# Where four per-sample norms are made: beside the attention windows or inside the spectra

## The chip, the cores and the metric

The kernel runs on one core of one Trainium2 chip. Its time is the device time of one execution, in microseconds (us): the median of 3 runs is 3876.3 us (3873.66 to 3883.53). The profiled execution has a span of 3873.3 us.

The core's engines each work through their own list of instructions and wait for one another through semaphores: TensorE (PE, matrix products), VectorE (DVE), ScalarE (ACT), GpSimd (POOL), and SyncE (SP), which issues most of the DMA transfers.

## The reference, cut to what matters

The program is a stack of four layers on an image tensor of 4 samples, 56 x 56 pixels, 128 channels. Layer 2 is a neural operator on the 56 x 56 token x channel images of each sample. It starts with two nested normalisations, a group norm over the sample (`_gn`, 32 groups of 4 channels) and an instance norm over the pixels of one image (`_inorm`), and then takes Fourier transforms of the normed images:

```python
x = x + _L0_conv_ref(_gn(x), ...)   # window attention, global attention, MLP
x = x + _L1_conv_ref(_gn(x), ...)   # edge layer
x = x + _L2_conv_ref(_gn(x), ...)   # spectral attention: the norms of this text
x = x + _L3_conv_ref(_gn(x), ...)

def _gn(v, G=32, eps=1e-5):
    g = v.reshape(B_, H_, W_, G, C_ // G)
    m = jnp.mean(g, axis=(1, 2, 4), keepdims=True)
    s = jnp.var(g, axis=(1, 2, 4), keepdims=True)
    return ((g - m) / jnp.sqrt(s + eps)).reshape(v.shape)

# in layer 2
def _inorm(x, g, b):
    m = jnp.mean(x, axis=(-2, -1), keepdims=True)
    v = jnp.var(x, axis=(-2, -1), keepdims=True)
    return (x - m) * jax.lax.rsqrt(v + EPS) * g + b
...
    xa_n = _inorm(xa, norm_g[0], norm_b[0])
    k = _fno_layer(xa_n, wK, wKs, bKs, (H // 2, W // 2))   # rfft2 of the image, products, irfft2
    q = _fno_layer(xa_n, wQ, wQs, bQs, (H // 2, W // 2))
    v = _fno_layer(xa_n, wV, wVs, bVs, (H, W))
```

## The kernel before

Layers 0 and 1 are computed for one sample after the other: 7x7 windows (`fast_windows`), global attention, MLP, edge layer. Their result of a sample stands in the tile x1 and is stored to x2d in DRAM. Then layer 2 begins for all samples at once, with the spectra. The branch used here is the one for small scores.

The two norms of layer 2 for one sample are a generator. Each `yield` ends one step, so that a caller can lay the steps between its own instructions. `bank()` gives a bank of PSUM, `xad` is the sample's place in DRAM.

```python
    x = xp[:, :HH, :]
    rows = wk.tile([P, HH, 6], F32, name="s_rows", bufs=1)
    for t in range(HH):
        nc.vector.bn_stats(rows[:, t, :], x[:, t, :])
        if t % 2 == 1:
            yield
    mv = wk.tile([P, 2], F32, name="s_mv", bufs=1)
    nc.vector.bn_aggr(mv, rows.rearrange("p a b -> p (a b)"))
    yield
    ps = bank()
    nc.tensor.matmul(ps[:, 0:1], k.g4, mv[:, 0:1], start=True, stop=True)
    yield
    mr = wk.tile([P, 2], F32, name="s_mr", bufs=1)
    t1 = wk.tile([P, 1], F32, name="s_t1", bufs=1)
    nc.vector.tensor_copy(mr[:, 0:1], ps[:, 0:1])
    nc.vector.tensor_sub(t1, mv[:, 0:1], mr[:, 0:1])
    nc.vector.scalar_tensor_tensor(t1, t1, t1, mv[:, 1:2], ALU.mult, ALU.add)
    yield
    ps = bank()
    nc.tensor.matmul(ps[:, 1:2], k.g4, t1, start=True, stop=True)
    yield
    var = wk.tile([P, 1], F32, name="s_var", bufs=1)
    nc.vector.tensor_copy(var, ps[:, 1:2])
    half = [rows[:, :, i] for i in range(6)]
    mean, sq, d = tiny("mean"), tiny("sq"), tiny("d")
    nc.vector.tensor_sub(d, half[1], half[4])
    yield
    nc.vector.tensor_mul(d, d, d)
    nc.vector.tensor_add(sq, half[2], half[5])
    yield
    nc.vector.scalar_tensor_tensor(sq, d, HH / 4, sq, ALU.mult, ALU.add)
    nc.vector.tensor_add(mean, half[1], half[4])
    yield "root"
    nc.scalar.activation(t1, var, AF.Sqrt, bias=k.eps)
    yield
    yield
    nc.vector.reciprocal(mr[:, 1:2], t1)
    nc.vector.tensor_scalar(mean, mean, 0.5, mr[:, 0:1], ALU.mult, ALU.subtract)
    nc.vector.tensor_scalar_mul(mean, mean, mr[:, 1:2])
    yield
    nc.vector.tensor_scalar(sq, sq, mr[:, 1:2], mr[:, 1:2], ALU.mult, ALU.mult)
    ps = bank()
    nc.tensor.matmul(ps[:, 64:64 + HH], k.ones_c, mean, start=True, stop=True)
    yield
    nc.vector.tensor_copy(st.norm[:, b, 0, :], ps[:, 64:64 + HH])
    nc.vector.tensor_sub(d, mean, st.norm[:, b, 0, :])
    yield
    nc.vector.tensor_mul(d, d, d)
    nc.vector.scalar_tensor_tensor(sq, d, float(HH), sq, ALU.mult, ALU.add)
    yield
    ps = bank()
    nc.tensor.matmul(ps[:, 128:128 + HH], k.ones_px, sq, start=True, stop=True)
    yield
    nc.vector.tensor_copy(d, ps[:, 128:128 + HH])
    yield
    for t in range(0, HH, 14):
        apply_norm(k, x[:, t:t + 14, :], x[:, t:t + 14, :], mr)
        if t == 42:
            nc.sync.dma_start(xad, x)
        yield "root" if t == 42 else None
    nc.scalar.activation(d, d, AF.Sqrt, bias=k.eps)
    yield
    yield
    nc.vector.reciprocal(d, d)
    nc.vector.tensor_scalar_mul(st.norm[:, b, 1, :], d, w.ng[:, 0:1])
    yield
```

Here `apply_norm` is one DVE instruction, recorded at line 193 (`tensor_scalar(out, xt, mr[:, 0:1], mr[:, 1:2], subtract, mult)`). The normed image replaces the raw one in place.

Before the change, the windows of sample b carry the steps of the norm of sample b - 1 (`beside` is this generator; a step follows each stage of the windows):

```python
# fast_windows
        steps = beside(bank)
        ...
        for n in range(NG + 11):
            for stage, g in ((norm, n + 2), (project, n), (score, n - 1), (value, n - 2), ...):
                if 0 <= g < NG:
                    stage(g)
                    step(False)
```

The spectra transform each sample along the channels (`first_transform`, four pieces of 14 tokens) and then along the tokens (`sample_spectra`, 13 parts: three s_ps, two blocks for R, eight s_px):

```python
# first_transform
    z = to[b] = wk.tile([P, 33, 2 * HH], F32, name="s_z")
    xf = x.rearrange("p t h -> p (t h)")
    for t0 in range(0, HH, 14):
        ps = psum.tile([P, 512], F32, tag="row", name="s_pr")
        for t in range(14):
            for ri in range(2):
                nc.tensor.matmul(ps[64 * ri:64 * ri + 64, t * 33:(t + 1) * 33],
                                 xf[:, (t0 + t) * HH:(t0 + t) * HH + 64], k.fw[:, ri, :], start=True, stop=True)
        nc.vector.tensor_mul(z[:, :, t0:t0 + 14], ps[:, :462].rearrange("p (t f) -> p f t", t=14),
                             bc(st.norm[:, b, 1, t0:t0 + 14], 1, 33))
        nc.scalar.copy(z[:, :, HH + t0:HH + t0 + 14], z[:, :, t0:t0 + 14])
        yield

# sample_spectra
    for c0, c1, v in C_BLOCKS_S:
        ps = psum.tile([P, 512], F32, tag="acc", bufs=4, name="s_ps")
        m = (c1 - c0) * HH
        nc.tensor.matmul(ps[:, :m].rearrange("p (c t) -> p c t", t=HH), k.fs[:, v, :], z[:, c0:c1, :HH],
                         start=True, stop=True)
        for dst, rows in ((st.S, slice(0, 64)), (st.iS, slice(64, P))):
            nc.scalar.copy(dst[o, b // 2, c0:c1, :HH], ps[rows, :m].rearrange("p (c t) -> p c t", t=HH))
        yield
    ...   # st.apart <- st.S, and two parts that write st.R
    for c0 in range(0, 32, 4):
        ps = psum.tile([P, 512], F32, tag="acc", bufs=4, name="s_px")
        for i in range(4):
            nc.tensor.matmul(ps[:112, i * 112:(i + 1) * 112], z[:, c0 + i, :], k.fx, start=True, stop=True)
        copy(k, c0 // 4, st.xh[:, b, :, c0:c0 + 4, :].rearrange("p i c r -> p c i r"),
             ps[:112, :448].rearrange("p (c i r) -> p c i r", c=4, i=2))
        yield

# spectra
        norm = normed_images(k, w, st, B - 1, wk, lambda: tiny.tile([P, 512], F32, name="s_pt"), st.x1, xad[B - 1])
        zs = {}
        first = [first_transform(k, st, b, (wk, psum), st.x1 if b == B - 1 else images(b), zs) for b in range(B)]
        for _ in first[0]:
            pass
        for b in range(B):
            for n, _ in enumerate(sample_spectra(k, st, b, (wk, psum), zs.pop(b))):
                for _ in range(3):
                    next(norm, None)
                if b < B - 1 and n in (2, 5, 7, 9):
                    next(first[b + 1])
```

The instructions of PE, ACT and DVE stand in the order of the program here. Those of other parts that are outside such a fixed order, like `conv_weights` (small DVE operations on weights, lines 1749 to 1775), are put between them by the program's scheduler.

Of the kernel before, what the change touches and what calls it, by code (L numbers as in the profile page):

```python
# [12 lines left out]
F32 = mybir.dt.float32  # L13
# [3 lines left out]
PSUM = bass.MemoryType.PSUM  # L17
DRAM = bass.MemoryType.DRAM

P = 128  # L20
B = 4
HH = 56
# [1286 lines left out]
def first_transform(k, st, b, pools, x, to):  # L1309

    nc = k.nc
    wk, psum = pools
# [13 lines that stand above are left out]
# [38 lines left out]
def spectra(k, w, st, xad, images):  # L1366

    nc, tc = k.nc, k.tc  # L1370
    for t in (st.S, st.iS, st.R):
        nc.gpsimd.memset(t[:, :, :, HH:], 0.0)
    nc.gpsimd.memset(st.x1[:, HH, :], 0.0)
    with ExitStack() as es:
        wk = es.enter_context(tc.tile_pool(name="s_wk", bufs=2))
        psum = es.enter_context(tc.tile_pool(name="s_ps", bufs=3, space=PSUM))
        tiny = es.enter_context(tc.tile_pool(name="s_pt", bufs=1, space=PSUM))
        es.enter_context(tc.manual_schedule(engines={mybir.EngineType.PE, mybir.EngineType.Activation,
                                                     mybir.EngineType.DVE}))
        norm = normed_images(k, w, st, B - 1, wk, lambda: tiny.tile([P, 512], F32, name="s_pt"), st.x1, xad[B - 1])  # L1380
        zs = {}
        first = [first_transform(k, st, b, (wk, psum), st.x1 if b == B - 1 else images(b), zs) for b in range(B)]
        for _ in first[0]:
            pass
        for b in range(B):
            for n, _ in enumerate(sample_spectra(k, st, b, (wk, psum), zs.pop(b))):
                for _ in range(3):
                    next(norm, None)
                if b < B - 1 and n in (2, 5, 7, 9):
                    next(first[b + 1])  # L1390


def value_weights(k, I, w, wk, dd):
# [1030 lines left out]
def build(k, packs, I, out):  # L2424


    nc, tc = k.nc, k.tc
    with ExitStack() as es:
        cp = es.enter_context(tc.tile_pool(name="const", bufs=1))
        dp = es.enter_context(tc.tile_pool(name="dram", bufs=1, space=DRAM))  # L2430
        x2d = dp.tile([B, P, HH, HH], F32, name="x2d")
        xad = dp.tile([B, P, HH, HH], F32, name="xad")
# [3 lines left out]
        x1w = x1p.tile([P, HH + 1, HH], F32, name="x1")  # L2436
# [4 lines left out]
        st = Env()  # L2441
        st.x1 = x1w
        st.norm = l2p.tile([P, B, 2, HH], F32, name="norm")
        with tc.tile_pool(name="w01", bufs=1) as wp, tc.tile_pool(name="io", bufs=1) as io:
            xw = io.tile([P, TOK], F32, name="xw")
            with ExitStack() as pre:
                xs = pre.enter_context(tc.tile_pool(name="i_x", bufs=B - 1))
                x = [xw] + [xs.tile([P, TOK], F32, name="i_x") for _ in range(B - 1)]
                w0, w1, w2 = Env(), Env(), Env()
# [35 lines left out]

            def norms(b, bank):

                if b < 0:
                    return iter(())
                return normed_images(k, w2, st, b, io, bank, x1w, xad[b])  # L2490

            with tc.If(small_scores > 0) as small:
                for b in range(B):
                    first_layers(lambda *a: fast_attention(*a, functools.partial(norms, b - 1), k.mr[:, b, :]), I["x"][b],
                                 x2d[b] if b < B - 1 else None, loaded=b == 0)
            with small.Else():
                with tc.For_i(0, B, 1) as b:
                    first_layers(functools.partial(both_attentions, beside=None),
                                 I["x"][bass.ds(b, 1)].rearrange("b p t -> (b p) t"),
                                 x2d[bass.ds(b, 1)].rearrange("b p l n -> (b p) l n"))  # L2500
                with tc.tile_pool(name="n_x", bufs=2) as xs, tc.tile_pool(name="n_ps", bufs=2, space=PSUM) as psum:
                    for b in range(B - 1):
                        xp = xs.tile([P, HH, HH], F32, name="n_x")
                        nc.sync.dma_start(xp, x2d[b])
                        for _ in normed_images(k, w2, st, b, io, lambda: psum.tile([P, 512], F32, name="n_ps"), xp,
                                               xad[b]):
                            pass

        x2s = ExitStack()
        x2p = x2s.enter_context(tc.tile_pool(name="x2", bufs=2, side="right"))  # L2510
# [1 line left out]
        def images(b):  # L2512
            if b not in loaded:
                xp = loaded[b] = x2p.tile([P, HH + 1, HH], F32, name="s_x2")
                for t in range(0, HH, 28):
                    nc.sync.dma_start(xp[:, t:t + 28, :], xad[b, :, t:t + 28, :])
                nc.gpsimd.memset(xp[:, HH, :], 0.0)
            return loaded[b]

# [54 lines left out]
```

## Time and profile before

| what | us |
|---|---|
| median of 3 runs | 3876.3 |
| span of the profiled run | 3873.3 |
| PE busy | 3546.0 (92%) |
| DVE busy | 2897.3 (75%) |
| ACT busy | 2077.8 (54%) |
| POOL busy | 1210.6 (31%) |
| windows of sample 0: first w_mm matmul to first f_s matmul | 55.23 to 155.06 |
| windows of sample 1 | 755.07 to 865.03 |
| windows of sample 2 | 1465.06 to 1575.02 |
| windows of sample 3 | 2178.53 to 2288.44 |
| spectra: first s_pr matmul to first q_acc matmul | 2888.70 to 2977.52 |

The names of tiles tell the stages: w_ is the windows, f_ global attention, m_ the MLP, e_ the edge layer, s_ the norms and the spectra, q_ the attention weights of layer 2. A line such as L1322 is the line of the kernel that made an instruction. A granted clock of 1.00 is PE's full speed.

### The profile page before, as it was taken

The page shows a single profiled execution, that of the slowest core. Times are in us where ns is not written, and L with a number is a line of the kernel's source. Part 1 is how long each engine was busy: PE and PEld are TensorE (multiplying, and loading weights), DVE is VectorE, ACT ScalarE, POOL GpSimd, SP SyncE. Part 2 cuts the span into 40 slices and gives each one's busy share as a digit, 9 for nine tenths or more (in the row PEclk, how much of TensorE's full clock was granted, in tenths as well). Part 3 has the DMA queues.
Part 4 walks back from the last instruction along what each step waited for, and adds up shares of the span by engine and source line. Part 5 has one row for each costly group of instructions (what it writes and reads, how often), then busy time and mean ns, then how long its engine had stood idle before and what let it go on. Part 6 is the DMA issues. An engine that isn't in the chain of part 4 may idle for free. (4 is left out here: it accounts for less than half of the span.)

```text
span 3873.3 us, 79430 instructions
## 1 busy us (share of the span) xinstructions
PE 3546.0 (92%) x35416; PEld 1589.1 (41%) x35416; DVE 2897.3 (75%) x2703; ACT 2077.8 (54%) x2080; POOL 1210.6 (31%) x667
## 2 busy tenths in 40 slices
PE   6899999989998998999989989999998989989988
PEld 4422234543322455322245532223456433336654
DVE  6588877859887786688869758887776767765664
ACT  4577765448776554677745457776542012214332
POOL 0000006600000570000028300000655769975555
PEclk8999999999999999999999999999998989998888
DMA  2000000000000000000000000000011058831101
GB/s 96 1 1 1 1 1 19 19 18 1 1 1 1 18 3 34 1 1 1 1 17 3 19 18 1 1 1 34 2 44 49 1 121 170 175 101 59 52 8 50
DMA packets 73496, 111.12 MB, mean 29 GB/s; under 512 B 62140, under 2 KB 63932, under 8 KB 67900
## 3 DMA queue, kind: packets, MB, share of 16 engines
q1 hardware_dynamic: 14460, 93.13, 8.0%
q10 hardware_dynamic: 58688, 12.85, 2.0%
q8 instruction: 279, 4.57, 0.5%
q14 instruction: 69, 0.57, 0.0%
HBM read 79.46 MB, written 26.51 MB: 27 GB/s over the span
## 5 line engine op out<-in xcount | busy, mean ns | idle before, releaser
L663 ACT ACTIVATE f_ring<-f_s 128x1792 f32<-128x1792 f32 (+3 forms) x796 | 1097.3, 1429 | 226.6 <-PE f_s L661 224.8
L606 DVE TENSOR_TENSOR f_acc<-f_acc,f_ring 128x1792 f32<-128x1792 f32 x560 | 1134.1, 2025 | 64.3 <-ACT f_ring L663 7.5
L661 PE MATMUL f_s<-f_qT,f_kT 32*128 32x448 f32 x5376 | 738.3, 572 | 47.9 <-ACT f_ring L663 27.9
L877 POOL TENSOR_TENSOR m_sq<-m_y 128x392 f32<-128x392 f32 x16 | 14.5, 919 | 1975.4 <-ACT m_y L876 1975.3
L612 PE MATMUL f_po<-f_ring,f_va 128*32 128x448 f32 x5376 | 589.8, 546 | 0.0
L1029 DVE TENSOR_TENSOR e_td<-e_pa,e_c 128x1792 f32<-128x1792 f32 x252 | 491.3, 2013 | 14.4 <-ACT e_a L994 14.4
L1031 POOL TENSOR_TENSOR e_tp<-e_a,e_c 128x1792 f32<-128x1792 f32 x140 | 451.8, 3257 | 145.1 <-PE e_acc L1036 104.4
L661 PEld LDWEIGHTS f_s<-f_qT,f_kT 32*128 32x128 f32 x5376 | 268.4, 183 | 524.5 <-ACT f_ring L663 378.9
L1036 PE MATMUL e_acc<-e_td,t_shared 32*32 32x448 f32 x8064 | 323.7, 546 | 22.0 <-DVE e_td L1029 10.9
L1033 ACT ACTIVATE e_tp<-e_tp 128x1792 f32<-128x1792 f32 x140 | 235.1, 1696 | 176.2 <-POOL e_tp L1031 176.2
L1645 DVE TENSOR_TENSOR u_ud<-u_px,u_d 112x1792 f32<-112x1792 f32 x144 | 240.1, 1708 | 96.4 <-PE u_po L1650 87.3
L612 PEld LDWEIGHTS f_po<-f_ring,f_va 128*32 128x32 f32 x5376 | 133.2, 109 | 396.3 <-issue 395.3
L1036 PE MATMUL e_acc<-e_tp,t_shared 32*32 32x448 f32 x4480 | 222.3, 547 | 3.2 <-ACT e_tp L1033 2.5
L1650 PE MATMUL u_po<-u_ud,AT 112*64 112x448 f32 x960 | 201.6, 550 | 23.3 <-DVE u_ud L1645 23.3
L1647 POOL TENSOR_TENSOR u_up<-xh,u_d 112x1792 f32<-112x1792 f32 x64 | 193.8, 3054 | 25.7 <-PE u_po L1650 12.4
L1036 PEld LDWEIGHTS e_acc<-e_td,t_shared 32*32 32x32 f32 x8064 | 134.1, 103 | 146.4 <-DVE e_td L1029 56.0
L629 DVE RECIPROCAL f_den<-f_den 128x448 f32<-128x448 f32 x28 | 82.7, 2953 | 77.2 <-ACT f_den L628 77.2
L1650 PE MATMUL u_po<-u_up,AT 112*64 112x448 f32 x576 | 126.9, 548 | 0.2
L1650 PEld LDWEIGHTS u_po<-u_ud,AT 112*64 112x64 f32 x960 | 64.9, 137 | 147.9 <-issue 86.7
L606 DVE TENSOR_TENSOR f_acc<-f_ring 128x1792 f32<-128x1792 f32 x28 | 56.7, 2025 | 86.6 <-ACT f_ring L663 57.7
L1512 POOL TENSOR_TENSOR q_u<-iS,q_g 128x1792 f32<-128x1792 f32 x32 | 102.7, 3237 | 56.2 <-PE s_px L1360 33.4
L1036 PEld LDWEIGHTS e_acc<-e_tp,t_shared 32*32 32x32 f32 x4480 | 95.2, 103 | 55.3 <-ACT e_tp L1033 19.4
(485 smaller groups left out, 4797.0 us busy)
## 6 DMA issues: line engine op xcount, KB each, us to landing
u_d<-dd SPq DMA_DIRECT2D x48, 784.0 KB
xw<-in_x SPq DMA_DIRECT2D x4, 1568.0 KB
x2d<-x SPq DMA_DIRECT2D x4, 1568.0 KB
xad<-x SPq DMA_DIRECT2D x4, 1568.0 KB
x_xs<-xad ACTq DMA_DIRECT2D x32, 196.0 KB
xm<-x_ev ACTq DMA_DIRECT2D x64, 98.0 KB
o_a<-xm SPq DMA_DIRECT2D x8, 784.0 KB
o_x<-x2d SPq DMA_DIRECT2D x4, 1568.0 KB
```

The costliest lines, as they stand in the source:

```text
L606: nc.vector.tensor_add(acc, slots(j, 0) if c == 1 else acc, slots(j, c))
L612: nc.tensor.matmul(po[heads[h], :NB], va[o, c, heads[h]], p, start=(c == 0), stop=(c == 24))
L661: nc.tensor.matmul(ss[:, i, :NB], kT[heads[h], c * P:(c + 1) * P], qT[heads[h], blk(j)], start=True, stop=True)
L663: nc.scalar.activation(ring[:, slot:slot + m, :], ss[:, :m, :NB], AF.Exp, scale=scale)
L1029: nc.vector.tensor_tensor(t, am, cm, ALU.max)
L1031: nc.gpsimd.tensor_sub(t, bc(a.rearrange("p (l n) -> p l n", l=8), 1, 4), cm)
L1033: nc.scalar.activation(tf, tf, AF.Relu)
L1036: nc.tensor.matmul(acc[quarters[q], r, :NB], k.ident[o, o], t[o, q].rearrange("p l n -> p (l n)"), start=(g == 0), stop=(g == len(EDGE_TUR ...
L1512: nc.gpsimd.tensor_mul(u, bc(st.iS[:, bp, c, :HH], 1, HEADS), bc(g[:, n, c, :], 2, HH))
L1645: nc.vector.tensor_mul(u, bc(px[:, :, :NB], 2, m), dm)
L1647: nc.gpsimd.tensor_mul(u, bc(x, 2, m), dm)
L1650: nc.tensor.matmul(po[64 * b2:64 * b2 + 64, :NB], st.AT[:, 8 * i + h0 + q, 2 * bp + b2, :], u[:, b2, q, :], start=(left == 16), stop=(left ...
```

## The change

The norms of samples 1, 2 and 3 move. Only the norm of sample 0 stays beside windows, those of sample 1. The other three are made inside the spectra, which now take the samples in the order 0, 3, 1, 2, so that sample 3, whose raw image still stands in x1, comes early, and each norm can be made in small steps while the sample before it is transformed. Three steps follow each piece of the first transform of sample 0, four follow each of the 13 parts of a sample; the first transform of the next sample moves from parts 2, 5, 7, 9 to parts 8 to 11, and ahead of it the norm that it needs is finished. Samples 1 and 2 are loaded raw from x2d rather than normed from xad, and are normed in place and stored to xad from there. It is meant to take the norms away from stages that they may hold up and to lay them where other work leaves room.

```diff
--- before.py
+++ after.py
@@ -1377,17 +1377,33 @@
         tiny = es.enter_context(tc.tile_pool(name="s_pt", bufs=1, space=PSUM))
         es.enter_context(tc.manual_schedule(engines={mybir.EngineType.PE, mybir.EngineType.Activation,
                                                      mybir.EngineType.DVE}))
-        norm = normed_images(k, w, st, B - 1, wk, lambda: tiny.tile([P, 512], F32, name="s_pt"), st.x1, xad[B - 1])
+
+
+        order = [0, B - 1, *range(1, B - 1)]
+
+        def of(b):
+            return st.x1 if b == B - 1 else images(b)
+
+        def steps(n):
+            for norm in norms[:1]:
+                for _ in range(n):
+                    if next(norm, norm) is norm:
+                        norms.pop(0)
+                        break
+
+        norms = [normed_images(k, w, st, b, wk, lambda: tiny.tile([P, 512], F32, name="s_pt"), of(b), xad[b])
+                 for b in order[1:]]
         zs = {}
-        first = [first_transform(k, st, b, (wk, psum), st.x1 if b == B - 1 else images(b), zs) for b in range(B)]
+        first = [first_transform(k, st, b, (wk, psum), of(b), zs) for b in order]
         for _ in first[0]:
-            pass
-        for b in range(B):
+            steps(3)
+        for i, b in enumerate(order):
             for n, _ in enumerate(sample_spectra(k, st, b, (wk, psum), zs.pop(b))):
-                for _ in range(3):
-                    next(norm, None)
-                if b < B - 1 and n in (2, 5, 7, 9):
-                    next(first[b + 1])
+                if i < B - 1 and 8 <= n < 12:
+                    while n == 8 and len(norms) + i >= B - 1:
+                        steps(1)
+                    next(first[i + 1])
+                steps(4)
 
 
 def value_weights(k, I, w, wk, dd):
@@ -2485,26 +2501,24 @@
 
             def norms(b, bank):
 
-                if b < 0:
+                if b != 1:
                     return iter(())
-                return normed_images(k, w2, st, b, io, bank, x1w, xad[b])
+                return normed_images(k, w2, st, 0, io, bank, x1w, xad[0])
 
             with tc.If(small_scores > 0) as small:
                 for b in range(B):
-                    first_layers(lambda *a: fast_attention(*a, functools.partial(norms, b - 1), k.mr[:, b, :]), I["x"][b],
+                    first_layers(lambda *a: fast_attention(*a, functools.partial(norms, b), k.mr[:, b, :]), I["x"][b],
                                  x2d[b] if b < B - 1 else None, loaded=b == 0)
             with small.Else():
                 with tc.For_i(0, B, 1) as b:
                     first_layers(functools.partial(both_attentions, beside=None),
                                  I["x"][bass.ds(b, 1)].rearrange("b p t -> (b p) t"),
                                  x2d[bass.ds(b, 1)].rearrange("b p l n -> (b p) l n"))
-                with tc.tile_pool(name="n_x", bufs=2) as xs, tc.tile_pool(name="n_ps", bufs=2, space=PSUM) as psum:
-                    for b in range(B - 1):
-                        xp = xs.tile([P, HH, HH], F32, name="n_x")
-                        nc.sync.dma_start(xp, x2d[b])
-                        for _ in normed_images(k, w2, st, b, io, lambda: psum.tile([P, 512], F32, name="n_ps"), xp,
-                                               xad[b]):
-                            pass
+                with tc.tile_pool(name="n_x", bufs=1) as xs, tc.tile_pool(name="n_ps", bufs=2, space=PSUM) as psum:
+                    xp = xs.tile([P, HH, HH], F32, name="n_x")
+                    nc.sync.dma_start(xp, x2d[0])
+                    for _ in normed_images(k, w2, st, 0, io, lambda: psum.tile([P, 512], F32, name="n_ps"), xp, xad[0]):
+                        pass
 
         x2s = ExitStack()
         x2p = x2s.enter_context(tc.tile_pool(name="x2", bufs=2, side="right"))
@@ -2513,7 +2527,7 @@
             if b not in loaded:
                 xp = loaded[b] = x2p.tile([P, HH + 1, HH], F32, name="s_x2")
                 for t in range(0, HH, 28):
-                    nc.sync.dma_start(xp[:, t:t + 28, :], xad[b, :, t:t + 28, :])
+                    nc.sync.dma_start(xp[:, t:t + 28, :], (x2d if b else xad)[b, :, t:t + 28, :])
                 nc.gpsimd.memset(xp[:, HH, :], 0.0)
             return loaded[b]
```

The last hunk is in `images(b)`, which loads a sample into one of two tiles for the spectra. The branch after `small.Else()` isn't the one that runs here.

## The prediction

> **What bounds the kernel now.** I read the page first: TensorE (PE) is busy 92% of the span, so a change to small VectorE (DVE) work can only matter where PE stands still for it. The norm of one sample (`normed_images`: 56 statistics, about 20 small operations, four in-place normalisations, four tiny matmuls) is such work. Before the change it lies in four places: beside the 7x7 windows of samples 1, 2 and 3 (norms of samples 0, 1, 2), and inside the layer 2 spectra (norm of sample 3). So I asked for the busy time by stage: the window stages, then the spectra cut at the marks of its samples. Columns: start:end, length, then busy time of PE, PE weight load, DVE, ACT and POOL, granted clock, DMA.
>
> ```profile
> core 0: us, PE busy (x) PEld busy (x) DVE busy (x) ACT busy (x) POOL busy (x), PEclk, DMA share, GB/s
> 55.00:155.00 100.00, 90.97 (x724) 55.58 (x724) 52.81 (x101) 47.64 (x80) 7.05 (x18) 0.94 0.00 1
> 755.00:865.00 110.00, 94.80 (x732) 57.19 (x732) 66.62 (x181) 48.12 (x82) 6.91 (x18) 0.92 0.07 28
> ...
> 2178.50:2288.40 109.90, 94.85 (x732) 57.24 (x732) 66.60 (x181) 48.13 (x82) 6.86 (x18) 0.92 0.07 28
> 2888.70:2896.20 7.50, 6.77 (x225) 6.66 (x225) 2.66 (x6) 1.80 (x4) 2.01 (x9) 1.00 0.91 304
> 2896.20:2926.70 30.50, 21.45 (x307) 18.90 (x307) 25.31 (x96) 8.52 (x19) 24.36 (x37) 0.78 0.34 115
> 2926.70:2948.30 21.60, 19.17 (x304) 16.09 (x305) 13.12 (x19) 7.60 (x17) 9.53 (x11) 0.84 0.28 109
> 2948.30:2964.80 16.50, 16.50 (x302) 14.60 (x301) 4.99 (x9) 7.70 (x17) 0.00 (x0) 1.00 0.02 5
> 2964.80:2977.50 12.70, 9.42 (x79) 7.77 (x77) 4.64 (x7) 7.31 (x16) 3.14 (x1) 1.00 0.13 34
> ```
>
> Two readings carry everything. The window stage without a norm takes 100.0 us, with one 110.0 us: 80 more DVE instructions, 13.8 us more DVE time, 10 us more on the path. And a sample of the spectra without a norm takes 16.5 us with PE busy throughout (the fourth spectra row), while the two samples that share the norm took 30.5 and 21.6 us.
>
> Next, why the norm costs time in the spectra. These are PE's and DVE's timelines there (start, length, operation, idle before it and its releaser).
>
> ```profile
> 2912.17 0.38 PE L1250 MATMUL s_pt<-s_mv,t_shared 128*128 128x1 f32 x2 [3.49 <-DVE s_mv L1247]
> ...
> 2920.73 0.58 PE L1259 MATMUL s_pt<-s_t,t_shared 128*128 128x1 f32 x2 [3.83 <-DVE s_t L1256]
> ...
> 2930.20 3.13 PE L1338 MATMUL s_ps<-s_z,t_images 128*128 128x448 f32 x4
> ```
>
> ```profile
> 2910.46 1.66 DVE L1247 BATCH_NORM_AGGREGATE s_mv<-s_rows 128x2 f32<-128x336 f32 x1
> ...
> 2918.51 0.94 DVE L1255 TENSOR_TENSOR s_t<-s_mv,s_mr 128x1 f32<-128x1 f32 x1
> 2919.49 1.18 DVE L1256 SCALAR_TENSOR_TENSOR s_t<-s_t,s_mv 128x1 f32<-128x1 f32 x1
> ...
> 2930.58 4.62 DVE L193 TENSOR_SCALAR x<-x,s_mr 128x784 f32<-128x784 f32 x4
> ```
>
> The norm is a chain DVE, PE, DVE, four times over. PE meets a tiny matmul of the norm, stands for 3.5 or 3.8 us, and the spectra's matmuls behind it stand too. From 2908.7 to 2933.3 us PE did about 6 us of the spectra's own work: the norm of sample 3 costs 19 us (30.5 + 21.6 - 2 x 16.55).
>
> [...] here the granted clock, asked for in 2 us steps, is 0.50 from 2914 to 2932 us, after the 3.49 us stand, and four s_ps matmuls then take 3.13 us. [...] The same four normalisations, in the groups of the window stage of sample 1 and of the spectra:
>
> ```profile
> L193 DVE TENSOR_SCALAR x<-x,s_mr 128x784 f32<-128x784 f32 x4 | 2.6, 679 | 0.0
> ```
>
> ```profile
> L193 DVE TENSOR_SCALAR x<-x,s_mr 128x784 f32<-128x784 f32 x4 | 4.6, 1214 | 0.0
> ```
>
> POOL works without a gap from 2902.1 to 2936.2 us (score and value weights), and L1255, 0.16 us in the window stage, takes 0.94 us here. Over the whole chain the excess is 0.8 (L1255) + 1.0 (L1256) + 0.4 (L1266) + 1.0 (L1272) + 0.3 (L1279) + 0.9 (L1286) + 0.9 (L1289) + 2.0 (L193) = 7.2 us.
>
> **The change, part by part.**
> (1) Windows of samples 2 and 3 lose their norm. First matmul to the first f_s matmul: 755.07 to 865.03 us with a norm, 55.23 to 155.06 us without: 110.0 against 99.8. Saved 2 x 10.1 = **-20.2 us**. Sample 0's norm stays beside sample 1.
> (2) Loads and stores keep their size: samples 1 and 2 are read from x2d instead of xad, and xad is written from the spectra. Stores of 1.6 MB have some 20 us until the next DMA that PE waits for. 0 us.
> (3) Norms of samples 1 and 2 inside the spectra. A norm has 50 steps (28 of two statistics, 29 the aggregate, 30 and 32 matmuls, 36 the root, 39 and 42 matmuls, 44 to 47 the normalisations). Four steps follow each of a sample's 13 parts. The first transform of the next sample now lies in parts 8 to 11, so steps 1 to 20 run there, PE having 9.65 us to do (four of 1.75, three of 0.88) and DVE less: hidden. The rest runs in parts 0 to 7, where PE has only 1.65 + 0.88 + 2.6 = 5.2 us. I count from the end of the last first-transform matmul. DVE: product 0.55, then statistics of parts 11, 12, 0, 1 (4 x 8 x 0.122 us from start to start), aggregate 1.6: ends at 6.1. PE is there after 0.88 + 1.65 = 2.5 and stands 3.6. Then the chain: round trips DVE to PE to DVE 0.60 + 0.68 + 0.85 + 0.76 = 2.9; small operations 0.52 + 1.04 + 0.41 + 0.99 + 0.14 = 3.1; the wait for the root behind ACT's R copies 0.85; one xh copy and the wait for it 0.95; four normalisations 2.4: ends at 16.4. PE then does its 9.65: period 26.05 instead of 16.55, so +9.5. A half clock in the stand of 3.6 us and the stop-and-go after it adds 0 to 3; I take 1.5. **+11 us a sample, +22**.
> (4) The norm of sample 3 is squeezed into sample 0's parts 0 to 8, while before it was spread to part 2 of sample 1. Transform 0 ends at 2895.4; DVE has 0.55 + 0.73 + 3.9 + 1.6 to do and the aggregate ends at 2902.2, just as POOL begins. The chain (two xh copies now) 11.0, POOL's share 7.2, and the small operations of `conv_weights` (L1750 to L1768), which I find on DVE from 2908 to 2917.8 in between, 6.7: 2927.1. Clock 1.5, then PE's 9.65: 2938.3. Unhindered it would be 2912, so 26 instead of 19: **+7 us**.
> Sum of the spectra: 2938.3 + 2 x 27.55 + 0.88 + 9.4 (sample 2 alone) + 3.3 (to the first q_acc) = 3007.0, against 2977.5 before: +29.5. With -20.2 the sum is +9.3 us. I shade this to +6: the place of `conv_weights` isn't in the diff, and in parts 8 to 12 or in DVE's gaps it would cost nothing (a third of 6.7 us).
>
> **Rivals.** First, the norms hide. The spectra have 66 us of PE work, and DVE's whole load there is 3 norms of 15.7 us, 20 us of its own work and 7 us of POOL's share: 75 to 85 us, no more than the 88.8 us that the stage takes today. Were latency no matter, the stage would not grow and the kernel would gain the full 20 us (3856). Against it: the two statistics rows above show PE standing in a chain, not DVE full. Second, the clock: if PE stays at 0.5 through each chain as it did from 2914 to 2932, its tiny matmuls and the xh blocks (1.83 instead of 0.97 us) lie in the chain as well and a norm costs 13 us: 3891. Third, the norms in the windows: if the 10 us there came from PE's clock at the place of the stage in the span, not from the norm, nothing would be saved; but three stages with a norm agree within 0.1 us. Fourth, the later xad stores could delay q_Tp's loads; q_u waited 1.35 us for one of them before, and 20 us lie between.
>
> **Range and chances.** -20.2 is firm to 1 us. The spectra's growth is not: +12 if the chain's fixed length is all that shows (5 + 5 + 2), +38 if the clock stays low and POOL hits harder. Middle +26, eight in ten from +13 to +38. Time: 3876.3 + 6, rounded to 3882; range 3868 to 3895. 2% is 77 us, nearly three times the largest growth, so within 2% is almost sure.
>
> **What would show it.** Window stages of samples 2 and 3 at 99.5 to 100.5 us, of sample 1 still 110. In the spectra, samples 0, 3, 1 at about 43, 27 and 27 us between their last first-transform matmuls, the last one at 9.4; s_pt L1250 with a stand of 3 to 4 us on DVE s_mv three times; L193 of sample 3 near 1.2 us each, of samples 1 and 2 near 0.68; a clock under 1 in each chain. I am wrong if PE's idle time there is under 6 us for a norm (then DVE ran ahead of my count), or if `conv_weights` has left the chain, or if attention after the spectra starts on another wait than q_u.

## The result and the profile after

The changed kernel takes **3909.1 us**, the kernel before 3875.0: a ratio of **1.0086, 95% interval 1.0069 to 1.0104**. That is within 2%, but 34 us more where the prediction had 6, and outside its range. Runs of one kernel lie up to 26 us apart here, so differences of medians under some 4 us are not read below.

I cut the profile after by stage, as the prediction did: the windows of samples 1, 2 and 3, then the spectra at the ends of the four samples' first transforms. The columns are as before: start:end, length, busy time of PE, PE weight load, DVE, ACT, POOL, granted clock, DMA.

```profile
758.02:868.38 110.36, 94.89 (x732) 57.18 (x733) 66.80 (x181) 48.17 (x82) 6.84 (x18) 0.92 0.07 28
1469.94:1566.57 96.63, 86.70 (x725) 54.87 (x725) 51.87 (x100) 47.73 (x80) 6.87 (x18) 0.98 0.04 16
2170.06:2268.28 98.22, 88.30 (x724) 55.02 (x725) 51.89 (x100) 47.74 (x80) 6.86 (x18) 0.97 0.04 15
2868.20:2884.60 16.40, 8.40 (x224) 8.22 (x224) 4.06 (x21) 1.74 (x3) 2.13 (x10) 0.79 0.98 367
2884.60:2937.40 52.80, 29.35 (x301) 26.15 (x301) 43.38 (x113) 8.03 (x18) 34.00 (x48) 0.58 0.28 101
2937.40:2967.70 30.30, 24.59 (x311) 20.98 (x309) 19.62 (x89) 8.53 (x19) 0.00 (x0) 0.72 0.14 55
2967.70:2998.20 30.50, 23.20 (x311) 19.94 (x309) 16.97 (x65) 8.44 (x19) 0.00 (x0) 0.78 0.14 55
2998.20:3011.80 13.60, 10.29 (x88) 8.59 (x86) 5.23 (x7) 7.69 (x17) 3.17 (x2) 1.00 0.12 33
```

The windows gave what was meant: 110 us with the norm, 97 and 98 without, and the spectra begin (end of the edge layer's last L1009) at 2868.2 instead of 2888.5 us, 20.3 us earlier. They then take 143.6 us to the first q_acc matmul, where before took 89.0: +54.6 instead of +29.5. The excess of 25 us lies in three rows: the first transform ends after 16.4 us (6.9 before), the part of sample 3 takes 52.9 (predicted 43), those of samples 1 and 2 take 30.3 and 30.5 (predicted 27.55). The last one, 13.6, is as predicted (9.4 + 0.88 + 3.3).

Three lines of PE's timeline say where PE stood (a stand is idle time of PE), and a fourth how slowly it then worked:

```profile
2875.98 5.99 PE L1322 MATMUL s_pr<-t_images,s_x 128*64 128x33 f32 x147 [8.60 <-DMA s_x<-xad]
...
2904.74 0.68 PE L1283 MATMUL s_pt<-s_mean,c_ones_c 128*128 128x56 f32 x2 [7.68 <-DVE s_mean L1279]
...
2917.35 0.67 PE L1292 MATMUL s_pt<-s_sq,c_ones_px 128*128 128x56 f32 x2 [10.35 <-DVE s_sq L1289]
...
2919.54 3.20 PE L1322 MATMUL s_pr<-t_images,x 128*64 128x33 f32 x56
```

The first stand waits for a load of an image. SyncE's timeline has that load behind one of weights, issued when the edge layer ended; before, it was issued over 200 us ahead of the spectra. First line before, then two lines after:

```profile
2673.28 2.02 SPq L2516 DMA_DIRECT2D s_x<-xad  x4
```

```profile
2867.52 0.81 SPq L158 DMA_DIRECT2D t_w_qk<-in_w_qk  x2
2868.45 1.78 SPq L2530 DMA_DIRECT2D s_x<-xad  x2
```

The other two stands wait for VectorE in sample 3's norm, and VectorE's timeline there has this, an operation on one column of 112 partitions (0.14 us in the kernel before):

```profile
2904.91 7.54 DVE L1766 TENSOR_TENSOR t_w_M<-t_w_M,t_w_M1rev 112x1 f32<-112x1 f32 x1
```

A VectorE operation that takes several us instead of its usual 0.1 to 0.7 is called caught or shut out below; the words say that it took long, not by what means, and "lock" in the expectations was a guess at the cause. So the suspects were: the order of SyncE's queue, GpSimd's hold on VectorE, PE's clock, and (since every step of the norm met the others) their interplay.

### The profile page after: what moved, and what is told of

Same layout as the page of the kernel before. It is cut to its first block, busy times and chain, and to the rows that moved or that the text cites. A ratio compares the mean times of both kernels' runs of the same rounds, so it can differ in the third digit from the quotient of the medians.

```text
span 3911.7 us, 79432 instructions
## 1 busy us (share of the span) xinstructions
PE 3562.4 (91%) x35416; PEld 1605.6 (41%) x35416; DVE 2906.8 (74%) x2703; ACT 2079.1 (53%) x2080; POOL 1211.4 (31%) x667
## 3 DMA queue, kind: packets, MB, share of 16 engines
q8 instruction: 280, 4.59, 0.5%
## 5 line engine op out<-in xcount | busy, mean ns | idle before, releaser
L877 POOL TENSOR_TENSOR m_sq<-m_y 128x392 f32<-128x392 f32 x16 | 14.6, 921 | 1956.6 <-ACT m_y L876 1956.5
L1663 POOL TENSOR_TENSOR u_up<-xh,u_d 112x1792 f32<-112x1792 f32 x64 | 193.9, 3055 | 26.0 <-PE u_po L1666 12.2
L1036 PEld LDWEIGHTS e_acc<-e_td,t_shared 32*32 32x32 f32 x8064 | 133.9, 103 | 147.1 <-DVE e_td L1029 56.7
```

The lines of the kernel that those rows point to most:

```text
L1036: nc.tensor.matmul(acc[quarters[q], r, :NB], k.ident[o, o], t[o, q].rearrange("p l n -> p (l n)"), start=(g == 0), stop=(g == len(EDGE_TUR ...
L1663: nc.gpsimd.tensor_mul(u, bc(x, 2, m), dm)
```

## The experiments

All medians beside runs of the kernel before, whose median was 3874.9 to 3875.8 us. The stretches of the spectra, in us: the first transform's end after the start, the part of the norm of sample 3, those of samples 1 and 2 (each to the end of the next first transform), the last sample to the first q_acc. In before, e4, e7, e9, e13 and e14 the order is 0, 1, 2, 3, so only the first transform and the total compare. The times are medians, the stretches come from one profiled run of each kernel, which can lie well off the median: e2's (3909.9 us) and e16's (3870.3 us) are the slowest of their kernels.

| kernel | time | first transform | 3 | 1 | 2 | last | spectra |
|---|---|---|---|---|---|---|---|
| before | 3875.0 | 6.9 | | | | | 89.0 |
| after | 3909.1 | 16.4 | 52.9 | 30.3 | 30.5 | 13.6 | 143.6 |
| e1 | 3900.0 | 15.1 | 45.6 | 29.2 | 30.4 | 13.6 | 133.9 |
| e2 | 3900.4 | 14.5 | 49.3 | 30.2 | 30.7 | 13.6 | 138.2 |
| e3 | 3892.1 | 20.8 | 34.6 | 29.0 | 30.2 | 13.6 | 128.2 |
| e4 | 3865.3 | 15.1 | | | | | 104.4 |
| e8 | 3899.4 | 6.9 | 57.6 | 29.0 | 30.2 | 13.6 | 137.4 |
| e9 | 3848.4 | 6.9 | | | | | 87.4 |
| e10 | 3885.6 | 11.8 | 36.3 | 29.1 | 30.3 | 13.6 | 121.1 |
| e15 | 3883.0 | 15.2 | 35.6 | 29.1 | 30.3 | 13.6 | 123.8 |
| e12 | 3877.4 | 6.9 | 34.9 | 29.0 | 30.2 | 13.6 | 114.7 |
| e5 | 3881.0 | 7.1 | 46.0 | 26.4 | 25.9 | 13.6 | 119.0 |
| e7 | 3870.7 | 6.9 | | | | | 90.7 |
| e11 | 3867.7 | 7.0 | 27.8 | 30.2 | 25.9 | 14.5 | 105.4 |
| e16 | 3858.6 | 7.0 | 27.9 | 25.9 | 25.9 | 14.6 | 101.4 |
| e13 | 3871.3 | 6.9 | | | | | 90.7 |
| e14 | 3867.6 | 6.9 | | | | | 81.4 |

### e1: the queue's order

The change also shortened the loop in the branch that never runs. Its last store was then to xad[0], and the compiler put the read of xad[0] later in SyncE's queue than before. That the one follows from the other was the guess; e1 has the old loop back.

```diff
-                    xp = xs.tile([P, HH, HH], F32, name="n_x")
-                    nc.sync.dma_start(xp, x2d[0])
-                    for _ in normed_images(k, w2, st, 0, io, ..., xp, xad[0]):
-                        pass
+                    for b in range(B - 1):
+                        xp = xs.tile([P, HH, HH], F32, name="n_x")
+                        nc.sync.dma_start(xp, x2d[b])
+                        for _ in normed_images(k, w2, st, b, io, ..., xp, xad[b]):
+                            pass
```

> The changed kernel with one thing put back: the body of the never-executed Else branch as it was before the change. Nothing that runs is altered, only the order in which the compiler lays the loads in SyncE's queue. Theory A (SyncE's queue order: the t_w_qk loads that wait for memory stand ahead of the s_x loads of the first transform, so the image arrives late): the s_x loads are issued some 200 us before the spectra as in the kernel before, the stand of 8.60 us at the first transform goes, and the kernel takes 9 to 10 us less than the changed one, about 3899.5 us. Theory B (the first transform waits for the last stores of the layer, whatever the queue order): the stand remains, 3909 us. A and B differ by over 8 us; the rest of the excess of the spectra (some 15 us over the predicted growth) stays in both.

3900.0 us, 9.2 less than the changed kernel, as theory A had it; but the total agrees partly by luck. The s_x loads were issued at 2652.4 us again and the stand of 8.60 us was gone, yet the first transform still ended at 15.1 us, only 1.3 us sooner. 7.3 us were gained in sample 3's part, where no VectorE operation took over 1.8 us this time. e1's timeline of PE shows another stand, at a moment that in after lay inside the wait for the image:

```profile
2868.42 0.27 PE L1322 MATMUL s_pr<-t_images,s_x 128*64 128x33 f32 x3 [1.00 <-DVE x L1009]
2871.33 11.96 PE L1322 MATMUL s_pr<-t_images,s_x 128*64 128x33 f32 x221 [2.63 <-issue]
```

PE stood 2.63 us for nothing that the profile shows ("issue"), and then did in 11.96 us what took 6.73 before. So the queue's order made the stand for the image; that it costs 9 us by itself is not shown.

### e2: the conv weights

```diff
-        load_weights(k, l3p, I, "w3_", w2)
-        load_weights(k, l3p, I, "w2_", w2, only=CONV_WEIGHTS)
...
                 x1s.close()
+                l3w = es.enter_context(tc.tile_pool(name="l3w", bufs=1, side="right"))
+                load_weights(k, l3w, I, "w3_", w2)
+                load_weights(k, l3w, I, "w2_", w2, only=CONV_WEIGHTS)
```

> e1 with one thing moved: the loads of the layer 3 conv weights, and so VectorE's 112x1 conv_weights operations, come after the first sample's norm instead of inside it. Theory A (small VectorE operations shut out while GpSimd issues without gap stand in sample 3's norm chain: 7.54 us for one of 112x1, and the conv_weights' 6.7 us): the first sample's part shrinks from 52.8 us to about 43 us and the kernel takes about 10 us less than e1, near 3889 us. Theory B (these operations only fill gaps in a chain that waits for TensorE at half clock and for ScalarE): no change against e1, within 1 us.

3900.4 us: no gain, as theory B said, though not for B's reason. In the profiled run, with conv_weights out of the chain, one of the norm's own operations was shut out: L1269, 128x56, took 6.79 us, and PE stood 11.67 us for L1283. So moving one group of operations away does not keep another from being caught.

### e3: GpSimd's arithmetic left out

> e1 with GpSimd's arithmetic for the value and score weights left out (only copies of the inputs stay, so the output is not the reference's). Theory A (GpSimd's run without gap from 2888.7 to 2922 us locks VectorE out and stretches the norm chain of the first sample): the first sample's part shrinks by 12 to 15 us, kernel near 3886 us, and the 112x1 operation returns from 7.54 us to about 0.15 us. Theory B (the chain is set by its own hand-offs and by TensorE's clock): 0 to 1 us less than e1, about 3899 us.

```diff
-    nc.gpsimd.tensor_add(half[:, 0, :], w.V[0:32, 0, 0, :], w.Vrev[:, 0, :])
-    ... (all of value_weights' and score_weights' arithmetic)
+    for n in range(3):
+        nc.gpsimd.tensor_copy(f[:, n], w.P[:, n % 2])
+    ... (and two copies for the score weights)
```

3892.1 us. Sample 3's part fell from 45.6 to 34.6 us, 11 of the 12 to 15 expected. VectorE was busy for 21.87 us in it instead of 35.02, for the same 113 operations: in e1 none had been caught for long, but many took longer. The edit did more than it was meant to: it also moved the image's loads, which were issued at 2854.3 us, 8 us ahead of the spectra instead of over 200. Two stands without a releaser at the start (2.2 and 6.2 us) gave nearly 6 us back.

### e4: the windows' gain alone

```diff
                 if b < 0:
                     return iter(())
+                if b > 0:
+                    nc.sync.dma_start(xad[b], x1)
+                    return iter(())
```

> The kernel before with the norms of samples 1 and 2 left out beside the 7x7 windows of samples 2 and 3, and put nowhere else (their factors are set to 1, so the output is not the reference's; the store of the sums stays). It measures the gain half of the change alone. The prediction's figure: 2 x 10.1 = 20.2 us less than the kernel before, 3855 us. The changed kernel's own windows: 13.3 + 11.7 = 25 us less, 3850 us. Rival (the windows' length does not come from the norm): 0 us, 3875 us.

e4 leaves the norms of samples 1 and 2 out altogether. 3865.3 us: 10 us less, half of the smaller figure. The windows were 26 us shorter than before, but the spectra 15 us longer (104.4), with nothing added in them: the stand of 2.46 us and the slow first transform were there too, and the operations of conv_weights, now at another moment of GpSimd's run, took 7.04 us once, for which PE stood 12.15 us. So a part of the loss belonged to any kernel with the two norms gone from the windows.

### e8 and e9: the program's length

In e1, e2 and e4 the stand came after exactly the fourth weight load of the first transform. After's profile lists a DMA queue of the kind "instruction" (280 packets, 4.59 MB: 16 KB each); in these runs its packet near this point had landed at 1.56, 1.03 and 1.53 us after the spectra's start, and the stand ended at 3.12, 2.53 and 2.94 us, each time 1.4 to 1.6 us later. And PE's program up to there had 28816 matmul records in all of them, against 28832 before: the two norms' eight matmuls, two records each. e8 is e1, e9 is e4, with eight that nothing reads:

```diff
+def pad_matmuls(k, bank):
+    ps = bank()
+    for i in range(4):
+        k.nc.tensor.matmul(ps[:, i:i + 1], k.g4, k.g4[:, 0:1], start=True, stop=True)
+    yield
...
+                if b > 1:
+                    return pad_matmuls(k, bank)
                 if b != 1:
                     return iter(())
```

> e1 with eight one-column matmuls that nothing reads added beside the windows of samples 2 and 3, four each, where the kernel before had its norms' eight. They give TensorE's program before the spectra the length that it had before the change (28832 matmul records instead of 28816). Theory A: in e1, e2 and e4 TensorE stood for 2.3 to 2.6 us with no releaser after the fourth weight load of the first transform, some 1.5 us past the landing of a 16 KB instruction transfer; the change shortened the program by 32 records and so put the end of such a transfer just there. With the old length the stand goes, the clock stays full, the first transform takes 6.7 instead of 12.2 us, and the kernel takes 7 to 9 us less than e1: 3892 us. Theory B: the stand comes from the loads' traffic at that moment, or is chance: 3900 us as e1, plus about 1 us for the eight matmuls.

> e4 (the kernel before, the norms of samples 1 and 2 left out) with the same eight one-column matmuls. e4's windows were 26 us shorter, but its spectra 15 us longer than before, though nothing was added in them. Theory A (the shifted instruction transfer and the half clock that follows made these 15 us): spectra back to about 89 us, kernel near 3850 us, 25 us less than before. Theory B (the spectra's growth belongs to the moved loads or to chance): 3865 us as e4.

e9: 3848.4 us, ratio 0.9929 (0.9906 to 0.9951), spectra 87.4: theory A to within 2 us. In e8 the stand went too, the first transform ended at 6.9 us at full clock, and yet the kernel took 3899.4. PE's and VectorE's timelines of e8 show where it went:

```profile
2868.37 6.73 PE L1329 MATMUL s_pr<-t_images,s_x 128*64 128x33 f32 x224 [1.00 <-DVE x L1009]
...
2908.32 0.68 PE L1290 MATMUL s_pt<-s_mean,c_ones_c 128*128 128x56 f32 x2 [19.90 <-DVE s_sq L1288]
```

```profile
2897.05 11.22 DVE L1286 TENSOR_SCALAR s_mean<-s_mean,s_mr 128x56 f32<-128x56 f32 x1
```

The norm of sample 3 now met GpSimd's run earlier, an operation of 0.25 us took 11.22, and PE stood 19.90 us. That the program's length moves the stand at the start was shown (e8 and e9 have none), what the stand costs was not; that stayed open until e15.

### e5 and e7: PE kept working

e5 is e8 with matmuls of 256 columns ahead of each norm matmul, in a bank of their own (one of the three row buffers); e7 is the kernel before with the same and with e2's edit.

```diff
+                for _ in range(((5, 5, 7, 3) if b == B - 1 else (6, 2, 5, 3))[i]):
+                    nc.tensor.matmul(spare[:, :256], k.fs[:, 0, :], k.fs[:, :2, :].rearrange(...), start=True, stop=True)
...
+    warm(0)
     nc.tensor.matmul(ps[:, 0:1], k.g4, mv[:, 0:1], start=True, stop=True)
```

> e8 with matmuls of 256 columns that nothing reads (3 to 7 of them, in a spare PSUM bank) ahead of each of the norms' matmuls in the spectra, so that TensorE works where it would stand. Theory A (the clock term of the prediction was mis-sized: TensorE at half clock costs 8 us in sample 3's part and some 3 us in each of the other two): the four transform pieces of sample 3's part take 1.82 instead of 3.20 us, and the kernel takes 8 to 14 us less than e8, 3878 to 3884 us. Theory B (the parts are set by VectorE's chain and GpSimd's lock, the clock only follows): no change against e8, or 2 to 4 us more for matmuls that stand in the way.

> A candidate: the kernel before, with the same matmuls (4 to 6) ahead of the four norm matmuls of its one norm in the spectra, and with the layer 3 conv weights loaded after that norm. If the half clock of 20.5 us in its spectra (24.7 to 45.2 us after their start) and the 5.8 us that its conv_weights stand between two steps of that norm cost what the theory says, it takes 4 to 8 us less than before, 3867 to 3871 us. Rival (e2's conv weights moved brought nothing): within 1 us of before.

e5: 3881.0 us, 18.5 less than e8. In samples 1 and 2 the mechanism is as expected: parts of 26.4 and 25.9 instead of 29.0 and 30.2, with the clock at 1.00 from 56.8 us after the spectra's start. In sample 3's part it is not: the four pieces still took 3.20 us each, not the 1.82 to 1.83 of the later samples' pieces, after PE had stood 4.60 us once more for a shut-out operation; the part is 11.7 us shorter than e8's with a smaller catch (3.83 us instead of 11.22), which the added matmuls don't explain. So only some 7 of the 18.5 us can be put down to them. e7: 3870.7 us (0.9987, 0.9977 to 0.9996), as expected by the time; but in its profiled run one operation was caught for 8.91 us and the spectra took 90.7 us, no less than before, so the profile does not show the gain.

### e10, e12 and e15: GpSimd placed elsewhere

e10 is e3 with the eight matmuls. e12 is e8 with all of GpSimd's work, but put in program order behind the norms:

```diff
+        def pool_work(b, n):
+            nc.gpsimd.tensor_copy(hold, st.norm[:, b, 1, 0:1])
+            for _ in itertools.islice(weights, n):
+                pass
...
                         norms.pop(0)
+                        pool_work(order[B - 1 - len(norms)], 18 if norms else 999)
```

> e8 with GpSimd's arithmetic for the value and score weights left out (only copies of the inputs stay, so the output is not the reference's): e3 again, but with the instruction transfer out of the way. In e3 sample 3's part was 34.6 us long instead of e1's 45.6, and two stands at the start (2.2 and 6.2 us) gave half of it back. In e8 a 128x56 operation of VectorE took 11.22 us while GpSimd issued without gap, and TensorE stood 19.90 us for it. Theory A (GpSimd's run without gap shuts VectorE out of sample 3's norm chain): no VectorE operation of the spectra over 3 us, no stand over 4 us, sample 3's part 33 to 37 us instead of 57.7, kernel 15 to 22 us below e8's, 3878 to 3884 us. Theory B (the chain's own hand-offs and TensorE's clock set the part): within 4 us of e8, 3896 to 3900 us.

> e8 with all of GpSimd's arithmetic kept, but placed: some 18 instructions wait for the norm of sample 3 to be done, 18 more for that of sample 1, the rest for that of sample 2, so that GpSimd's run falls beside the transform pieces and not beside the norm chains. Theory A (the lock is what costs): as e10, 3878 to 3884 us, plus at most 3 us for what lies beside the transforms. Theory B: 3896 to 3900 us. If the late weights are wanted before they are done, a new wait appears at the first product of the attention weights.

> e12 without the eight one-column matmuls, so with the instruction transfer's end four weight loads into the first transform again, and GpSimd's run still behind the norms. Theory A (that stand costs its 2.5 us and, by the half clock after it, another 5 us of first transform): 7 to 9 us more than e12, 3884 to 3886 us, first transform ended at 15 us instead of 6.9. Theory B (what e8 showed is all: the shift is worth nothing): within 2 us of e12, 3877 us.

e10: 3885.6 us, theory A with a small miss. Sample 3's part is as expected, but the first transform took 11.8 us instead of e8's 6.9: PE stood 2.19 and 1.21 us there without a releaser, although the eight matmuls are in. As in e3 the edit had moved the image's loads, to 2859.5 us.

e12: 3877.4 us, 22 below e8, with the same arithmetic done. Sample 3's part in e8 and then in e12, columns as above:

```profile
2875.10:2932.70 57.60, 29.37 (x301) 26.17 (x301) 44.55 (x113) 8.01 (x18) 32.28 (x48) 0.57 0.29 105
```

```profile
2876.60:2911.60 35.00, 27.80 (x303) 24.66 (x301) 21.97 (x113) 8.03 (x18) 12.19 (x20) 0.68 0.41 146
```

The same 113 VectorE operations took 21.97 us instead of 44.55, none of them over 2.3 us. So the gain does not need the arithmetic to be gone, only to be elsewhere.

e15, without the eight matmuls: 3883.0 us, first transform ended at 15.2 us. Behind the stand the granted clock was 0.50, from 2868.0 to 2884.0 us. So the stand and the half clock behind it cost 8.3 us in the profile and 5.6 in the medians. GpSimd's run cost 10 us in sample 3's part by e1 against e15, and 22.7 by e8 against e12. The medians of e1 and e15 differ by 17 us; the other 7 lie ahead of and behind the spectra and are not explained.

### e11, e13, e14 and e16: both repairs

e11 is e5 with e12's order and e2's late conv weights; e13 is the same for the kernel before; e16 and e14 are e11 and e13 with the conv weights loaded as before.

> A candidate: e5 (TensorE kept working ahead of the norms' matmuls) with GpSimd placed as in e12 and the layer 3 conv weights loaded after the spectra. If clock and lock are the two causes and independent, sample 3's part falls from e5's 46 us to about 26.4, as those of samples 1 and 2 in e5 (26.4 and 25.9), the spectra from 119 to about 100 us, and the kernel to 3858 to 3864 us, 11 to 17 us less than the kernel before. Rival (the starved operation only moves to the next norm, or the late weights hold up what follows): 3872 to 3881 us as e5.

> e7 (the kernel before with matmuls ahead of its norm's matmuls and late conv weights) with GpSimd's arithmetic after that norm. Its spectra had one VectorE operation of 8.91 us and one stand of TensorE of 7.29 us. If the lock made them, the spectra fall from 90.7 to about 80 us and the kernel from 3870.7 to 3859 to 3864 us; then the change of place of the norms brings nothing beyond what these two repairs bring to the kernel before. Rival (they fill time that TensorE's work needs anyway): 3868 to 3871 us.

> The kernel before with two repairs and nothing else: matmuls ahead of the four norm matmuls, and GpSimd's arithmetic after that norm; conv weights loaded as before. In e13 the transforms ended at 64.9 us instead of 74.0, and an 8.75 us stand for conv_weights, which waited for a late load, took that back. If that load was the cause, the spectra take 79 to 82 us instead of 89 and the kernel 3863 to 3867 us. Rival (the stand is the late GpSimd run itself): 3870 to 3872 us as e13.

> e11 with the conv weights loaded as before: the moved norms with the same two repairs as e14. If the late conv weights did no harm in e11, within 2 us of it, 3866 to 3870 us, with conv_weights' operations at 0.15 us each in sample 3's part. Against e14: if the move of the norms is worth its 20 us in the windows less three parts of 26 us instead of 16.6 (10 us each, 20 for the two moved norms), the two are alike within 4 us; if moving is worth more, e16 is 5 us or more below e14.

e11: 3867.7 us, between the two theories: sample 3's part fell to 27.8 us, but the late conv weights, or what came with them, cost some 9 us against e16. e13: 3871.3, the rival's figure; its transforms ended 9 us earlier than before, then PE stood 8.75 us behind this operation, the first of conv_weights, in VectorE's timeline of e13:

```profile
2969.36 0.36 DVE L1806 TENSOR_SCALAR t_w_W<-t_w_W 128x384 f32<-128x384 f32 x1 [12.67 <-DMA t_w_W<-in_w_W]
```

e14, without that: 3867.6 us, ratio 0.9982 (0.9974 to 0.9991), spectra 81.4. e16: **3858.6 us, ratio 0.9958 (0.9942 to 0.9974)**. Both take less than either kernel of the change. e16's spectra by sample:

```profile
2867.00:2874.20 7.20, 6.66 (x224) 6.64 (x224) 4.31 (x22) 1.73 (x3) 0.65 (x4) 1.00 0.94 334
2874.20:2902.10 27.90, 26.03 (x343) 22.30 (x340) 21.73 (x113) 7.88 (x18) 6.77 (x16) 1.00 0.51 179
2902.10:2928.10 26.00, 25.00 (x347) 21.74 (x343) 19.54 (x89) 8.43 (x19) 11.31 (x24) 1.00 0.17 66
2928.10:2954.00 25.90, 24.90 (x343) 21.68 (x341) 16.89 (x65) 8.43 (x19) 7.91 (x9) 1.00 0.16 65
```

The clock is 1.00 in every row, and POOL's time is spread over them. Whether the move itself is now worth something is not settled: by the medians e16 is 9 us below e14, with intervals that meet at 0.9974, but in the two profiled runs its spectra are 20.0 us longer and begin only 16.8 us earlier. e16's profiled run, 3870.3 us, was the slowest of its six, e14's took 3864.3, so the profiles are harder on e16 than the medians.

## Why the prediction was wrong

From after to e16 the medians go 3909.1, 3900.0 (e1, queue), 3883.0 (e15, GpSimd), 3877.4 (e12, the program's length), 3858.6 (e16, clock): 9, 17, 6 and 19 us. In the profiled runs the spectra shrink at these steps by 9.7, 10.1, 9.1 and 13.3 us; some 8 of the 50 us lie elsewhere in the kernel and are not explained. What each cause costs also depends on which of the others are still there. Against the prediction's steps:

- **Step 1, the windows: the mechanism held; that the net agrees to 0.1 us is luck.** -20.2 predicted, -20.3 at the spectra's start. The stages themselves gave 13.3 and 11.7 us; sample 0's stage, which I took as the measure of a stage without a norm, ran at a clock of 0.94, samples 2 and 3 now at 0.98 and 0.97. The other 5 us were lost in samples 0 and 1, where the change alters nothing. e9, with nothing else in the way, gave 27 us.
- **Step 2, "Loads and stores keep their size ... 0 us": failed.** Size was not the question, order was. An edit in a branch that never runs put the image's load behind one that was issued only at 2867.52 us, when the edge layer ended, and PE stood 8.60 us. With the old order alone the first transform gained 1.3 us, since PE then stood 2.63 us without a releaser and took 11.96 us for the rest; with both mended (e8) it ended at 6.9 instead of 16.4 us, 9.5 us sooner.
- **Step 3, the norms of samples 1 and 2: the chain was right, the clock term was mis-sized.** The chain gave a period of 26.05 us; e16, at full clock, has 25.9 and 25.9. The 1.5 us of half clock that I added were an estimate; after has 30.3 and 30.5, at clocks of 0.72 and 0.78, so it is over 4; e16 against e12, which differ only in the added matmuls and their bank, gives 3.1 and 4.3. The second rival named this and put a norm at 13 us; the periods here less 16.55 are 13.8 and 13.9.
- **Step 4, sample 3's norm: the unhindered part was right, its hindrances were mis-sized.** Without POOL's 7.2, conv_weights' 6.7 and the clock's 1.5 the predicted 43 becomes 27.6; e16 has 27.9. The hindrances together were 25 us, not 15.4: the four pieces took 17.8 instead of 9.65 us at half clock (0.50 from 2919.5 to 2937.4 us), 8 us, and GpSimd's run took the other 17 (52.9 against e15's 35.6). The 7.2 came from adding up the excess of the kernel before, operation by operation, as if it came out the same each time. It is a draw, not a price: 7.54 us on one operation here, 7.04 in e4, 11.22 in e8, none over 2.3 us before; and e1 lost its 10 us with none over 1.8.
- **Shading to +6: wrong direction.** conv_weights stayed in the chain, and moving them (e2) brought nothing.
- **Not in the prediction at all:** that taking 32 records out of PE's program brings a stand of 2.0 to 2.8 us into the first transform (e1, e2, e4, e15), and a clock of 0.50 behind it (e4, e15). In after its moment lay inside the 8.60 us for the late image; once that was mended it cost 6 us (medians) to 8 us (first transform), by e15 against e12.
- **The signs.** Of those that I said would show me wrong, conv_weights gone and another wait after the spectra didn't come. PE idle under 6 us for a norm came once, barely: 23.5, 5.7 and 7.3 us, the 5.7 beside work of PE's that a clock of 0.72 made longer. L193 came out as said, 4.97 us for sample 3's four and 2.47 and 2.48 for the others'; L1250's stand of 3 to 4 us came twice (3.29, 1.99, 3.59). The signs missed the size of a stand: the clearest mark of trouble in the profile is the s_pt stand of 10.35 us, three times the 3 to 4 I had named.
- **One reading was off, without weight for the sum.** 77 us is twice the largest growth given for the spectra (38), not nearly three times.

## What to carry to other kernels

A chain of small hand-offs between VectorE and TensorE should not share its time with a GpSimd program that runs without a gap: sample 3's part took 57.6 us beside it (e8) and 34.9 with it elsewhere (e12). Price such an overlap by its worst draw, or order GpSimd behind the chain, as e12 did for 22 us at no loss of work. Where TensorE must stand for such a chain, give it wide matmuls to do there: with them the parts of samples 1 and 2 fell from 29.0 and 30.2 us (e12) to 25.9 and 25.9, at a clock of 1.00 (e16). And look at the granted clock of the work that follows, not only at the stand: in e1 a stand of 2.63 us was followed by 11.96 us for work that had taken 6.73. Before pricing a move, compare the order of each DMA queue and the length of each engine's program in the two kernels: neither can be read off the diff, and here the one made a stand of 8.60 us (after) and the other 5.6 us of time (e15 against e12). The same holds for an experiment: e3 and e10 moved loads that they were not meant to touch.

## What the hardware showed that I had not expected

**A VectorE operation was out for as long as many GpSimd instructions in a row.** In e8 an operation of 0.25 us took 11.22 us; sixteen GpSimd instructions started in that time, none of which took over 1.39 us. In the changed kernel it was twelve in 7.54 us, none over 1.40 us. With GpSimd's work behind the norms (e12) none of the same 113 operations took over 2.3 us. How the one holds up the other is not shown.

**A busy PE did not always get its clock back.** In e4, after the stand of 2.46 us, PE was busy for 12.2 us with matmuls of 33 columns at 0.50 throughout; the clock was back only behind the s_ps matmuls of up to 448 columns. The clock is the last column but two:

```profile
2865.10:2877.30 12.20, 12.16 (x221) 11.89 (x220) 1.92 (x3) 1.73 (x3) 1.28 (x5) 0.50 0.69 236
2877.90:2881.50 3.60, 3.47 (x8) 1.62 (x8) 2.20 (x19) 2.03 (x5) 3.60 (x8) 0.52 1.00 375
2881.50:2890.30 8.80, 8.80 (x199) 8.01 (x198) 5.99 (x34) 3.81 (x8) 8.60 (x13) 1.00 0.20 77
```

In e10 the clock did return among the same matmuls, after 3.3 us of them:

```profile
2870.10:2873.40 3.30, 3.30 (x63) 3.30 (x64) 0.00 (x0) 0.00 (x0) 0.00 (x0) 0.50 1.01 419
2873.50:2875.10 1.60, 1.60 (x57) 1.60 (x55) 1.35 (x8) 0.58 (x1) 0.00 (x0) 1.00 0.81 258
```

So their width is not what decides it; what does is open. In e8 the same matmuls kept the full clock that they found, 224 of them in 6.73 us.

**PE stood just behind the landing of 16 KB of instructions.** With 32 records fewer ahead of it, a stretch of weight loads some 30 ns apart (224 in 6.64 us where it did not stand, before) stood 2.0 to 2.8 us (e1, e2, e4, e15), in e1, e2 and e4 until 1.4 to 1.6 us after such a landing; with the old length it did not (e8, e9, e12). The length alone does not settle it: e10 has the old one and stood 2.19 and 1.21 us at two other places, 1.7 and 1.4 us after such a landing. That the instructions were what PE waited for is inferred from the landing times; the profile names no releaser.
